# The order of work around the first block, and the place of one addend in the last batch entry, in a fused attention and FP4 feed-forward kernel

## The chip, the cores and the metric

The kernel runs on one core of a Trainium2 chip. A core has five engines, each with its own queue of instructions: TensorE (PE, matrix products), VectorE (DVE), ScalarE (ACT), GpSimd (POOL) and SyncE (SP, which issues the DMAs here). The metric is the device time of one execution in microseconds (us), as a median over runs.

## The reference, cut to what matters

The input `src` has 4 batch entries of 2048 rows of 256 values. Each row is normalized to `xn`, and two paths work on it: linear attention with a feed-forward layer, and a feed-forward layer in which each matrix product quantizes both of its operands to FP4 in groups of 16 values. The second is the gate of the first.

```python
xn = layernorm(src)
# path 1: linear attention (16 heads of 64), then an MLP
Q, K = elu(xn @ Wq + bq) + 1, elu(xn @ Wk + bk) + 1;  v = xn @ Wv + bv
KV = einsum('bshd,bshm->bhdm', K, v)          # sums over all 2048 rows of a batch entry
Z  = 1 / (einsum('bshd,bhd->bsh', Q, K.sum(1)) + 1e-6)
o  = einsum('bshd,bhdm,bsh->bshm', Q, KV, Z)
x1 = layernorm(xn + o @ Wo + bo) * g1 + be1
s  = layernorm(x1 + gelu(x1 @ W1 + b1) @ W2 + b2) * g2 + be2
# path 2: fp4(t) = round each group of 16 to a grid of 8 levels times its scale max|t|/6
h  = silu(fp4(xn) @ fp4(w_gate).T) * (fp4(xn) @ fp4(w_up).T)     # 704 wide
g  = silu(fp4(h) @ fp4(w_down).T)
return src + s * g
```

## The kernel before, in words

Rows are taken in blocks of 256 (two tiles of 128), 8 blocks to a batch entry, 32 in all. Attention of a batch entry needs the sums over all of its keys first. So an intro (L966 to L1025) computes the keys of entry 0, tile by tile, and each block of entries 0 to 2 computes beside its own work a share of the next entry's keys. The last entry, blocks 24 to 31, has no next keys; its blocks are shorter and have an order of their own.

*From keys to M.* Per half of the heads, `m_of_half` (L540 to L615) folds the sums of keys and values with Wv and Wo into a matrix M, so that a block needs only one product with its queries (`pa`, L825). It is a generator of steps: load Wv and Wo (one buffer each, so the second half's load of Wo waits for the first half's product with it); the key sums as a row (`pks`), through memory to all partitions (`ksum`); then `kcol` and `kh`; `pkv` and `kv`; and `pm`, which ACT copies to `m`. `step(gen, k)` runs k steps of such a generator.

*A block's FP4 path.* The scales of groups of x and h (`scales_x`, `scales_h`, L631 and L650) are made on DVE for block n while block n−1 runs. `spread_scales` (L666) transposes the scales on PE (`pscale`), ACT copies them (`scaleT`), SP stores them to memory and reads them back with eight broadcasting DMAs into `qT`. `grid_of_x` and `grid_of_h` round to the grid, `grid_T` (L683) transposes it by a DMA into `gridT`, and `quantized_x` and `quantized_h` (L691, L697) multiply the two on DVE: `qT` then holds the quantized operand. x of block n+1 and h of block n go through this together. From `qT`, `gate_up(n+1)` (`pg`, 32 matmuls, L702) makes the next block's h, and `down(n)` (`pd`, L727) this block's gate: ACT makes `g` by a silu, and `o` and `x` are allotted beside it, `x` loaded.

*A block's attention path.* `q_of` (`pq`, L763) makes `zq`, the queries; `sums` (L791) makes `pz`, its reciprocal `z`, and spreads it by memory to `zb`; `qz` (L818) multiplies `zq` by `zb`; `attention` makes `pa` and `x1`; `x1_T` transposes it (`pt_x`), `ffn_1` (`pf`), `ffn_2` (`py`) and `output` (L924) follow, the last two in the next block. `output` ends with two `scalar_tensor_tensor` that write `o` and take the addend in `o` and `g`.

*The weights.* w_gate and w_up are quantized tile by tile within the intro. w_down has two halves, `quantize_down(w, k)` (L350): maxima, scales, rounding on DVE and ACT over 128x704, then six transposes on PE (`pwd`) and copies by ACT to `wd`; the generator stops between these. W2 is multiplied in a form with fewer products, which needs four sums or differences of its quarters: `w2_sums` (L193), four POOL operations over 128x512. In the intro the quarters are loaded with tile 5 (`later`).

*POOL's addends.* POOL keeps the key sums (`kacc`), the small powers that make `rstd` (L379), and the addends: `gate_addend` (L748: `o = g·be2 + x`, `g = g·g2`, three passes over 128x512), `ffn_addend` (L755, two passes over x1) and `attention_addend` (xn + bo).

*What sets the order.* PE runs strictly in program order (L98 to L102). DVE and ACT do so until `in_order[0] = False` (L1046); behind that a scheduler orders DVE, ACT, POOL and SP by readiness, within explicit hints:

```python
with tc.issue_after(pool["last"]) if behind else nullcontext():   # L750
```

puts what stands in it behind the named instruction; `pool["last"]` is the last POOL addend issued so far. With `behind=False` the scheduler is free. The transition from intro to block 0 (L1026 to L1056) is an order written out by hand: the steps of w_down's quantization, of `gate_up(0)` and of M lie in each other's gaps.

Of the kernel before, what the change touches and what calls it, by code (L numbers as in the profile page):

```python
# [22 lines left out]
def linear_attention_gated_by_fp4_ffn(  # L23
# [40 lines left out]
    ND = D // P  # L64
# [128 lines left out]
    def w2_sums():  # L193
        nc.gpsimd.tensor_tensor(w2("t3"), w2("22"), w2("t1"), ALU.subtract)
        nc.gpsimd.tensor_tensor(w2("t1"), w2("t1"), w2("11"), ALU.subtract)
        nc.gpsimd.tensor_tensor(w2("t2"), w2("22"), w2("t1"), ALU.subtract)
        nc.gpsimd.tensor_tensor(w2("t4"), w2("21"), w2("t2"), ALU.subtract)
# [152 lines left out]
    def quantize_down(w, k):  # L350
        yield from quantize_weight(w[:, k, :], I, f"wd_{k}")
        for i0 in range(0, NI, 4):
            n = min(4, NI - i0)
            pt = mm_tile(f"pwd_{k}_{i0}")
            for i in range(n):
                cols = slice((i0 + i) * P, min((i0 + i + 1) * P, I))
                wide = cols.stop - cols.start
                tr(pt[:wide, i * P : (i + 1) * P], w[:, k, cols], ident)
            for lo, hi, rows_ in ((0, n, P),) if i0 + n < NI else ((0, n - 1, P), (n - 1, n, TAIL)):
                scalar.copy(  # L360
                    wd[:rows_, i0 + lo : i0 + hi, k * P : (k + 1) * P],
                    pt[:rows_, lo * P : hi * P].rearrange("p (i t) -> p i t", t=P),
                )
        yield


    pool = {}
# [282 lines left out]
    def scales_h(n, j):  # L650
        blk[n]["rs_h", j] = fp4_scale(blocks(blk[n]["h"][j]), scale[:, : I // BLK, j], f"h_{n}_{j}")

    def grid_of_h(n, j, issue=None):
        h3 = blocks(blk[n]["h"][j])
        fp4_grid(
            h3, blk[n].pop(("rs_h", j)), h3, [(blocks(grid_h[:, j, :I]), 0, I // BLK)],
            f"h_{n}_{j}", issue,
        )
# [7 lines left out]
    def spread_scales(n, h, x):  # L666

        cs = chunks_of(h, x)
        wide = cs.stop - cs.start
        ptT = mm_tile(f"pscale_{n}")[:, :P]  # L670
        tr(ptT, scale.rearrange("p k j -> p (k j)"), ident)
        sT = work.tile([P, P], F32, tag="scaleT", name=f"scaleT_{n}", bufs=1)
        scalar.copy(sT, ptT)
        s_d = dram.tile([P, P], F32, tag="scale_d", name=f"scale_d_{n}", bufs=2)
        nc.sync.dma_start(s_d, sT)
        by_block = s_d.rearrange("(c k j) t -> k c (j t)", c=NCH, j=TB)
        for k in range(P // BLK):
            nc.sync.dma_start(
                qT[k * BLK : (k + 1) * BLK, cs, :],
                by_block[k : k + 1, cs, :].to_broadcast([BLK, wide, T]),  # L680
            )
# [63 lines left out]

    def gate_addend(n, behind=True):  # L748
        g, o, x = (blk[n][k] for k in ("g", "o", "x"))
        with tc.issue_after(pool["last"]) if behind else nullcontext():  # L750
            nc.gpsimd.tensor_tensor(o, g, rows["be2"], ALU.mult)
            nc.gpsimd.tensor_tensor(o, o, x, ALU.add)
            pool["last"] = nc.gpsimd.tensor_tensor(g, g, rows["g2"], ALU.mult).ins
# [198 lines left out]
    def step(gen, times=1):  # L952
        for _ in range(times):
            next(gen, None)
# [70 lines left out]
            xn = xn_next  # L1025
    load_xn(1)  # L1026
    load_xnT(0)
    down_0, down_1 = (quantize_down(w_down_sb, k) for k in range(ND))
    step(down_0)
    step(gate, 2)  # L1030
    step(m_0)
    step(down_0)
    step(gate, 2)
    step(m_0)
    step(down_0)
    scales_x(1)
    step(gate)
    step(m_0)
    step(gate)
    scales_h(0, 0)  # L1040
    m_half = m_of_half(0, 1)
    step(m_half)
    step(gate, 9)
    step(m_0)
    scales_h(0, 1)
    in_order[0] = False  # L1046
    step(down_1)
    for sub in range(2):
        keys_in(1, sub)
    spread_scales(0, True, True)  # L1050
    step(down_1)
    w2_sums()
    for j in range(TB):
        grid_of_h(0, j)
    grid_of_x(1)
    grid_T(0, 0, NCH * TB)  # L1056

# [4 lines left out]
    def keys_beside(n):  # L1062
        return n // NB + 1 < B
# [10 lines left out]
    for n in range(NBLK):  # L1074
        b, bi = divmod(n, NB)
        subs = (2 * bi, 2 * bi + 1) if b + 1 < B else ()
        if n < last:
            gate = gate_up(n + 1)
        for sub in subs if n == 0 else ():
            keys_T(b + 1, sub)  # L1080
        if n > 0 and keys_beside(n - 1):
            gate_addend(n - 1)
        if subs:
            step(m_half)
            q_of(n)
            step(down_1)
            load_xnT(n + 1)
            kk_ins = keys_k(b + 1, subs[0])
            block_addends(n)
            with tc.issue_after(kk_ins):  # L1090
                ins = quantized_x(n)
            with tc.issue_after(sums(n, ins.ins).ins):
                for j in range(TB):
                    quantized_h(n, j)
            if n > 0:
                keys_T(b + 1, subs[1], keys["exp"])
            step(m_half)
            keys_xk(b + 1, subs[0])
            step(gate, 9)
            step(m_half)  # L1100
            down(n, 0)
            down(n, 1)
        elif n < last:
            def values():
                quantized_h(n, 0)
                return quantized_x(n)

            step(m_half)
            q_of(n, values)
            block_addends(n)  # L1110
            quantized_h(n, 1)
            load_xnT(n + 1)
            down(n, 0)
            sums(n)
            step(m_half)
            step(gate, 9)
            step(m_half)
            down(n, 1)
            gate_addend(n, False)
        else:  # L1120
            for j in range(TB):
                quantized_h(n, j)
                down(n, j)
        with tc.issue_after(blk[n + 1]["late"]) if n < last else nullcontext():
            qz_ins = qz(n)
        if not subs:
            ffn_2(n - 1, 4 if n < last else 8)
        kk_ins = keys_k(b + 1, subs[1]) if subs else qz_ins
        if n > 0:
            with tc.issue_after(kk_ins):  # L1130
                ffn_sums(n - 1)
        attention(n)
        if n + 2 < NBLK:
            load_xn(n + 2)
        if subs:
            keys_xk(b + 1, subs[1])
            if subs[1] % NB == NB - 1:
                m_half = m_of_half(b + 1, subs[1] // NB)
                step(m_half)
        bn, bin_ = divmod(n + 1, NB)  # L1140
        next_subs = (2 * bin_, 2 * bin_ + 1) if bn + 1 < B else ()
        for sub in next_subs if n > 0 else ():
            keys_in(bn + 1, sub)
        if n > 0:
            ffn_2(n - 1, 20)
        more = n + 1 < NBLK, n + 2 < NBLK
        if more[0]:
            scales_h(n + 1, 0)
            with tc.issue_after(qz_ins) if not subs else nullcontext():
                scales_h(n + 1, 1)  # L1150
            if more[1]:
                scales_x(n + 2)
        for sub in next_subs if n == 0 else ():
            keys_in(bn + 1, sub)
        for sub in next_subs[:1]:
            keys_apart(bn + 1, sub)
        if n == last:
            gate_addend(n)
        x1_T(n)
        if not subs:  # L1160
            ffn_addend(n, n == last)
        for sub in next_subs[1:]:
            keys_apart(bn + 1, sub, blk[n]["act"])

        if n > 0 and not subs:
            ffn_2(n - 1, 26)
        if more[0]:
            spread_scales(n + 1, *more)
        if n > 0:
            ffn_2(n - 1, 28)  # L1170
        if more[0]:
            grid_of_h(n + 1, 0)
            grid_T(n + 1, 0, NI)
            grid_of_h(n + 1, 1, blk[n]["act"])
            if more[1]:
                grid_of_x(n + 2, blk[n]["act"])
                if not subs:
                    attention_addend(n + 2, False)
            grid_T(n + 1, NI, (NCH if more[1] else NI) * TB)
        if n > 0:  # L1180
            output(n - 1)
        if n + 1 == last:
            q_of(last)
            ffn_1(n, range(NF // 2))
            sums(last)
            ffn_1(n, range(NF // 2, NF))
        else:
            ffn_1(n)
        for sub in next_subs[:1]:
            keys_T(bn + 1, sub, blk[n]["gelu"])  # L1190
# [38 lines left out]
```

## Time and profile before

| what | value |
|---|---|
| median of 3 runs | 1930.21 us (1927.91 to 1932.57) |
| the profiled execution | 1929.81 us |
| its span in the profile | 1927.7 us |
| mean granted TensorE clock | 0.996 |
| PE busy, of the span | 1892.9 us |
| DVE busy | 1495.7 us |
| POOL busy | 561.1 us |
| block 0's `pg` starts (intro's end) | 131.37 us |
| block 1's `pg` starts | 172.31 us |
| block 0's `pd` starts | 183.58 us |
| last block's `pf` starts | 1905.56 us |

In the lines of the profile a name such as `pg<-wgu,qT` is output and inputs by the program's tiles, followed by shapes and a count of equal neighbours that are shown as one line. The number ahead of the engine is the duration, or the stretch that all of them took; the bracket is the engine's idle time just before, and what ended it. L115 is the line of the helper through which all of DVE's and ACT's instructions are issued, L99 and L102 those of matmuls and transposes, so there the tile's name tells the place. "Granted clock" is the share of full speed that TensorE was given: at 0.5 a matmul takes twice its time.

### The profile page before, as it was taken

How to read it: one execution, taken by the hardware profiler on the slowest of the kernel's cores; microseconds unless marked ns; L12 is line 12 of the kernel's file. 1: busy time of each engine (PE TensorE's matmuls, PEld its weight loads, DVE VectorE, ACT ScalarE, POOL GpSimd, SP SyncE). 2: the span in 40 equal slices, each digit the busy share in tenths (PEclk: the TensorE clock that was granted, in tenths of full speed). 3: DMA queues.
4: the chain of work that ended last, by engine and by line, in shares of the span. 5: the costliest groups of instructions: out<-in, count | busy, mean ns of one | idle time of the engine just before them, and what ended most of it. 6: DMA issues, size and time to landing. Idle time of an engine off the chain costs nothing. (4 is left out here: it accounts for less than half of the span.)

```text
span 1927.7 us, 24464 instructions
## 1 busy us (share of the span) xinstructions
PE 1892.9 (98%) x8788; PEld 1380.7 (72%) x8788; DVE 1495.7 (78%) x2554; ACT 803.0 (42%) x1384; POOL 561.1 (29%) x461
## 2 busy tenths in 40 slices
PE   9999999999999999999999999999999999999997
PEld 4446677767777767777767777767777678788876
DVE  7878687777778877877777878877778788788775
ACT  2334554334444345443334554444443334444441
POOL 4441332232332233322232323232323232222221
PEclk9999999999999999999999999999999999999999
DMA  5435555454435445535244554455343244455431
GB/s 160 140 94 119 115 104 113 97 107 94 93 59 98 117 94 119 142 73 107 78 89 75 126 111 96 96 115 120 82 88 70 62 87 82 86 90 89 85 78 36
DMA packets 225121, 187.12 MB, mean 97 GB/s; under 512 B 103364, under 2 KB 185568, under 8 KB 225000
## 3 DMA queue, kind: packets, MB, share of 16 engines
q1 hardware_dynamic: 224168, 183.99, 45.0%
q8 instruction: 69, 1.13, 0.3%
q10 hardware_dynamic: 832, 1.57, 0.3%
q14 instruction: 52, 0.43, 0.1%
HBM read 131.41 MB, written 31.54 MB: 85 GB/s over the span
## 5 line engine op out<-in xcount | busy, mean ns | idle before, releaser
L508 POOL TENSOR_TENSOR kacc<-kacc,kk 128x512 f32<-128x512 f32 x120 | 178.9, 1491 | 591.2 <-DVE kk L115 589.1
L99 PE MATMUL pg<-wgu,qT 128*128 128x352 f32 x1024 | 310.4, 461 | 0.8 <-issue 0.3
L99 PEld LDWEIGHTS pg<-wgu,qT 128*128 128x128 f32 x1024 | 193.2, 190 | 119.9 <-issue 14.2
L99 PE MATMUL pxk<-kk,xn_k 128*128 128x512 f32 x512 | 237.7, 603 | 3.7 <-DVE kk L115 3.5
L99 PE MATMUL pa<-m,zq 128*128 128x256 f32 x1024 | 227.9, 380 | 5.2 <-DVE zq L115 5.2
L99 PE MATMUL pk<-wk_sb,xnT_k 128*128 128x512 f32 x512 | 230.4, 593 | 1.4 <-ACT xnT_k L115 1.0
L99 PE MATMUL pq<-xnT,wq_sb 128*128 128x256 f32 x1024 | 227.0, 380 | 0.2 <-ACT hT L115 0.2
L99 PE MATMUL pf<-x1T,w_sb 128*128 128x256 f32 x1024 | 227.0, 380 | 0.0
L379 POOL TENSOR_TENSOR rstd<-rstd,neg_half 128x2 f32<-128x2 f32 x96 | 73.0, 760 | 526.8 <-DVE rstd L115 477.6
L99 PEld LDWEIGHTS pa<-m,zq 128*128 128x128 f32 x1024 | 193.4, 190 | 43.8 <-issue 12.0
L99 PEld LDWEIGHTS pq<-xnT,wq_sb 128*128 128x128 f32 x1024 | 194.9, 191 | 27.1 <-ACT hT L115 0.6
L99 PEld LDWEIGHTS pf<-x1T,w_sb 128*128 128x128 f32 x1024 | 192.4, 190 | 25.6 <-issue 0.4
L115 ACT ACT_TABLE_LOAD x122 | 156.5, 1283 | 68.1 <-DVE k L115 55.3
L99 PE MATMUL pd<-wd,qT 128*128 128x256 f32 x768 | 172.3, 379 | 1.5 <-DVE qT L115 1.5
L99 PEld LDWEIGHTS pxk<-kk,xn_k 128*128 128x128 f32 x512 | 92.7, 190 | 110.3 <-issue 77.1
L99 PEld LDWEIGHTS pk<-wk_sb,xnT_k 128*128 128x128 f32 x512 | 97.2, 190 | 103.5 <-issue 96.8
L99 PEld LDWEIGHTS pd<-wd,qT 128*128 128x128 f32 x768 | 145.8, 190 | 25.9 <-DVE qT L115 2.3
L115 DVE SCALAR_TENSOR_TENSOR zq<-e,q 128x512 f32<-128x512 f32 x128 | 88.8, 704 | 70.2 <-ACT e L115 70.2
L115 ACT ACTIVATE h<-pg 128x352 f32<-128x352 f32 x128 | 58.7, 459 | 192.9 <-PE pg L99 192.8
L115 ACT ACTIVATE x1T<-pt_x,bcol 128x256 f32<-128x256 f32 x64 | 32.6, 560 | 255.4 <-PE pt_x L102 255.4
L115 ACT ACTIVATE ek<-k,neg_one 128x512 f32<-128x512 f32 x128 | 89.8, 719 | 113.1 <-DVE k L115 112.7
L115 ACT ACTIVATE hT<-pf,bcol 128x256 f32<-128x256 f32 x256 | 105.2, 471 | 67.0 <-PE pf L99 66.6
(133 smaller groups left out, 2824.9 us busy)
## 6 DMA issues: line engine op xcount, KB each, us to landing
zb<-z_d SPq DMA_DIRECT2D x128, 256.0 KB, 6.1
qT<-scale_d SPq DMA_DIRECT2D x248, 128.0 KB, 5.4
x_k<-in_L_attn_src_dram SPq DMA_DIRECT2D x32, 256.0 KB, 4.3
x<-in_L_attn_src_dram SPq DMA_DIRECT2D x32, 256.0 KB, 2.7
xn_d<-xn_k SPq DMA_DIRECT2D x32, 256.0 KB, 3.7
xn<-xn_d SPq DMA_DIRECT2D x32, 256.0 KB, 2.7
xnT_d<-xnT_k SPq DMA_DIRECT2D x32, 256.0 KB, 2.0
xnT<-xnT_d SPq DMA_DIRECT2D x32, 256.0 KB, 3.1
```

The source lines that it names most:

```text
L99: return tc.keep_in_program_order(nc.tensor.matmul(*args, **kw))
L115: ins = op(*args, **kw)
L379: pool["last"] = nc.gpsimd.tensor_tensor(rstd[:, j0:j1], rstd[:, j0:j1], neg_half[:, j0:j1], ALU.pow).ins
L508: acc = nc.gpsimd.tensor_tensor(kacc, kacc, kk, ALU.add)
```

## The change

It moves instructions and adds or removes none, and consists of four pieces.

1. *Transition.* All eight steps of `gate_up(0)` and block 0's scales now stand ahead of the second half of M's first products and ahead of all of w_down's quantization. M's first half stops before `pm`, which moves into block 0 behind `q_of`.
2. *Block 0.* w_down's quantization follows `quantized_x` there, by a hint, its transposes stand just ahead of `down(0)`. `keys_T` comes behind `q_of`.
3. *W2's sums* move from the transition (where the scheduler had placed them in the intro, as soon as W2 had arrived) into block 0 behind the addends.
4. *Last batch entry.* `gate_addend(n)` of blocks 24 to 30 was called at the end of block n's own `down`, without a hint; it is now called at the head of block n+1, behind the last POOL addend. In block 31, `x1_T` and `ffn_addend` come ahead of `gate_addend`, and `ffn_addend` is without a hint.

```diff
-    def gate_addend(n, behind=True):
+    def gate_addend(n):
         g, o, x = (blk[n][k] for k in ("g", "o", "x"))
-        with tc.issue_after(pool["last"]) if behind else nullcontext():
+        with tc.issue_after(pool["last"]):
...
-    down_0, down_1 = (quantize_down(w_down_sb, k) for k in range(ND))
-    step(down_0)
-    step(gate, 2)
+    down_steps = [quantize_down(w_down_sb, k) for k in range(ND)]
+
+    step(gate, 4)
     step(m_0)
-    step(down_0)
-    step(gate, 2)
-    step(m_0)
-    step(down_0)
+    scales_h(0, 0)
     scales_x(1)
-    step(gate)
-    step(m_0)
-    step(gate)
-    scales_h(0, 0)
+    step(gate, 4)
+    scales_h(0, 1)
     m_half = m_of_half(0, 1)
     step(m_half)
-    step(gate, 9)
-    step(m_0)
-    scales_h(0, 1)
+    step(m_0, 2)
+    spread_scales(0, True, True)
     in_order[0] = False
-    step(down_1)
     for sub in range(2):
         keys_in(1, sub)
-    spread_scales(0, True, True)
-    step(down_1)
-    w2_sums()
     for j in range(TB):
         grid_of_h(0, j)
+    step(m_half)
     grid_of_x(1)
     grid_T(0, 0, NCH * TB)
...
-        for sub in subs if n == 0 else ():
-            keys_T(b + 1, sub)
-        if n > 0 and keys_beside(n - 1):
+        if n > 0:
             gate_addend(n - 1)
         if subs:
-            step(m_half)
+            if n > 0:
+                step(m_half)
             q_of(n)
-            step(down_1)
+            if n == 0:
+                for sub in subs:
+                    keys_T(b + 1, sub)
+                step(m_0)
...
             block_addends(n)
+            if n == 0:
+                with tc.issue_after(pool["last"]):
+                    w2_sums()
             with tc.issue_after(kk_ins):
                 ins = quantized_x(n)
...
+            with tc.issue_after(ins.ins):
+                for g in down_steps if n == 0 else ():
+                    step(g, 2)
...
             step(gate, 9)
             step(m_half)
+            for g in down_steps if n == 0 else ():
+                step(g)
             down(n, 0)
             down(n, 1)
...
             down(n, 1)
-            gate_addend(n, False)
...
+        x1_T(n)
+        if not subs:
+            ffn_addend(n, False)
         if n == last:
             gate_addend(n)
-        x1_T(n)
-        if not subs:
-            ffn_addend(n, n == last)
```

## The prediction

> **What bounds the kernel now.** First the page's busy times:
>
> ```profile
> PE 1892.9 (98%) x8788; PEld 1380.7 (72%) x8788; DVE 1495.7 (78%) x2554; ACT 803.0 (42%) x1384; POOL 561.1 (29%) x461
> ```
>
> TensorE (PE) is idle for 1927.7 − 1892.9 = 34.8 us of the span, and the change touches no matmul. So it can win only such idle time, or time lost at a lowered clock, and the question is where both lie. The windows of 50 us on PE give: 6.4 us idle in 100–150, 2.5 in 150–200, some 1.5 in all of 200–1550, 10.7 in 1550–1900, 10.2 in the last 28. These are the places that the change touches: the transition into block 0, and the last batch entry (blocks 24 to 31). The timeline of PE, then those of SP, POOL and DVE, say what ends each gap. Transition:
>
> ```profile
> 151.84 0.48 PE L102 MATMUL pscale<-ident,scale 128*128 128x128 f32 x1 [3.81 <-DVE scale L115]
> 172.31 9.71 PE L99 MATMUL pg<-wgu,qT 128*128 128x352 f32 x32 [0.31 <-issue]
> ```
> ```profile
> 155.09 3.73 SPq L678 DMA_DIRECT2D qT<-scale_d  x8
> 163.03 2.69 SPq L687 DMA_TRANSPOSE gridT<-grid  x1
> ```
>
> Columns: start, duration, engine, line, operation, in brackets the idle time ahead and its releaser. Read: a stall of 3.81 us for the scales of block 0, and later a start of pg(1), block 1's gate matmuls, with no stall: the transposed grid (gridT) was there. The windows on PE show what such a stall costs besides (columns: window, length, PE busy, granted clock, DMA share, GB/s):
>
> ```profile
> 114.00:117.40 3.40, 3.40 (x5) 0.52 0.55 208
> 151.80:155.00 3.20, 3.16 (x12) 0.50 0.18 64
> 1889.00:1893.00 4.00, 3.82 (x17) 1.00 0.00 1
> 1902.00:1905.50 3.50, 3.44 (x19) 0.61 0.00 0
> ```
>
> They follow stalls of 2.64, 3.81, 1.58 and 1.45 + 1.01 us (with one short transposing between the last two). The Trainium skill ("TensorE: Matmul & The Clock Gate", section "Part 1: The HAM clock gate (the "warmup" mystery)") puts the price at an idle window of about 3.4 us. By that rule only the 3.81 would be charged; the rows charge the 2.64 and the split 2.5 too, so I take 2.5 as the point from which some 3.4 us at half clock, 1.7 us lost, must be expected.
>
> **Step 1, W2's four sums leave the intro.** They stand on POOL between the key sums and a rstd that DVE waits for:
>
> ```profile
> 102.62 1.60 POOL L197 TENSOR_TENSOR w_sb<-w_sb 128x512 f32<-128x512 f32 x1
> 104.19 1.15 POOL L379 TENSOR_TENSOR rstd<-rstd,neg_half 128x2 f32<-128x2 f32 x1
> ```
> ```profile
> 84.20 0.69 DVE L115 TENSOR_TENSOR k<-pk,bk 128x512 f32<-128x512 f32 x1 [0.88 <-PE pk L99]
> 91.14 0.68 DVE L115 SCALAR_TENSOR_TENSOR kk<-ek,k 128x512 f32<-128x512 f32 x1
> ...
> 98.90 0.69 DVE L115 TENSOR_TENSOR k<-pk,bk 128x512 f32<-128x512 f32 x1 [3.09 <-PE pk L99]
> 108.16 0.68 DVE L115 SCALAR_TENSOR_TENSOR kk<-ek,k 128x512 f32<-128x512 f32 x1
> ```
>
> From the first k to the third kk the tile before took 6.94 us, this one 9.26: **2.3 us** are the sums' price (queue on POOL, and stretched DVE operations beside them). In the intro DVE is the chain up to pg at 131.37, so I carry all of it. Bounds: 0 (other work fills it) to 3. Behind the attention addends of block 0 POOL stands idle in before from 173.2 to 194.3, and takes the four passes (1.27 each) there; beside DVE they stretch one or two operations, 0.6 us, counted in step 2.
>
> **Step 2, the transition and block 0.** I use before's clock of time, unshifted. In front of the scales PE now has all eight gate groups, pks and pkv, no w_down transposes. From pg at 131.37: four times eight gates at 2.5 from start to start, two pks at 0.95, pkv at 1.1, so PE is through at 144.4. The scales on DVE need the last gate (142.4), h 0.52, its maximum 0.88 and a scaling 0.18, with ACT and queueing about 144.9 (w_down's quantization no longer stands between): a gap of 0.5, too short to lower the clock, instead of 3.81. Then pscale 0.3, pq 7.1 (the page's 227.0/32 at full clock), pt_k 1.2, pm_0 1.9, so 155.4; then pk 3.7, pz 1.0, pkv 1.1, pxk 3.6 (less the overlaps): PE reaches pg(1) at 164.5 instead of 172.3.
>
> But SP now carries a new wait. In the built order the load of Wo for the second half stands between the second and third of the eight qT broadcasts, and it needs the one Wo buffer, free when pm_0 ends (155.4); before, that load was issued at 148.06 ahead of the whole chain. Behind it queue six broadcasts and the gridT transpose. Six issues at 3.73/8 take 2.8 us, so gridT is issued at 158.7. In before it was issued at 163.03 and its consumer, the qT product on DVE, started at 171.21: 8.2 us. That gives 166.9, and with 0.9 for the product 167.8. The last batch's chain shows 9.3 for the same transfer: 168.0. So PE stands 3.3 us before pg(1), above my 2.5: half clock behind it.
>
> What is late next is w_down: both halves' quantization (ten passes over 128x704 at 0.82 to 0.88 us, two small reciprocals) now follows quantized_x on DVE, mixed with z (0.42 + 1.75), qT (1.76) and the h products. Added row by row, w_down's first half is done 13.95 us behind gridT, the second 16.05, and 0.6 for the sums beside them: 183.55. Six transposes (0.82) and the copy by ACT put pd at 184.8, against 183.58 for pd in before: **+1.2**; with the 9.3 us transfer +2.3. The half clock under pg(1) is hidden by that DVE train. I take **+1.7**. Bounds: −4.6, if gridT's wait vanishes and w_down follows in time; +5, if pd starts at half clock behind stalls of 1.6 and 1.9 us and the train is stretched.
>
> **Step 3, the gate addend of blocks 24 to 30 moves into the next block.** In before its three POOL passes run while DVE makes zq, and PE waits for zq (block 26):
>
> ```profile
> 1711.56 1.22 DVE L115 TENSOR_TENSOR zq<-zq,zb 128x1024 f32<-128x1024 f32 x1 [1.01 <-DMA zb<-z_d]
> 1713.93 2.29 DVE L115 TENSOR_TENSOR zq<-zq,zb 128x1024 f32<-128x1024 f32 x1
> 1716.29 5.45 PE L99 MATMUL pa<-m,zq 128*128 128x256 f32 x24 [0.69 <-DVE zq L115]
> ```
>
> Beside POOL the second zq takes 2.29 for 1.22, and the gaps before pa are 0.63, 0.69, 0.56, 0.74 and 1.05 us at 1670, 1715, 1760, 1806 and 1853: **3.7 us** to win. In its new place the addend stands behind the rstd of the previous block's output, beside the o pair. Three batches of before show that place already:
>
> ```profile
> 270.54 2.89 DVE L115 SCALAR_TENSOR_TENSOR o<-s,rstd,o 128x256 f32<-128x256 f32 x2 [0.58 <-POOL rstd L379]
> ...
> 1691.66 0.88 DVE L115 SCALAR_TENSOR_TENSOR o<-s,rstd,o 128x256 f32<-128x256 f32 x2 [0.59 <-POOL rstd L379]
> 1694.83 0.96 DVE L115 TENSOR_TENSOR qT<-qT,gridT 128x768 f32<-128x768 f32 x1 [2.28 <-DMA qT<-scale_d]
> ```
>
> Here the Trainium skill speaks against the change ("SBUF — State Buffer", section "Who interferes with whom": a VectorE instruction with two SBUF inputs contends with a GpSimd one that reads SBUF, and whoever is second is blocked for the whole instruction). By the rule alone the collision is only moved: each of the two o passes could wait one POOL pass of 1.40 us, +2.8 per block, about what was won or more. The row says +2.0 (2.89 against 0.88), and behind the pair DVE stands idle for 2.03 to 4.28 us before its next qT product. That idle time takes the 2.0; what remains is a qT or a zq caught by the last pass. Block by block I estimate 0.4, 0, 0.15, 0.4, 0.5 and 0 for 25 to 30, and 1.0 to 1.3 for 31 (1871.66), where three zq follow at once and delay pz: **2.75**. Bounds: 0, or 2.0 in each of seven blocks.
>
> **Step 4, the last block's tail.** POOL now takes x1's passes ahead of the gate's, so x1's normalization loses its neighbour:
>
> ```profile
> 1899.32 2.68 DVE L115 TENSOR_SCALAR x<-x,mv,rstd 128x256 f32<-128x256 f32 x2 [0.21 <-POOL rstd L379]
> 1902.06 0.55 PE L102 MATMUL pt_x<-ident,x 128*128 128x128 f32 x3 [1.01 <-DVE x L115]
> ```
>
> Elsewhere that pair takes 0.73 (1679.30): −1.95. The split stall then falls under 2.5, and the half clock behind it, 1.25 more, goes: pf from 1905.56 to about 1902.4, **−3.2**, at least −1.95. The gate's passes end well before the last output needs them.
>
> **Sum.** −2.3 + 1.7 − 3.7 + 2.75 − 3.2 = −4.7. The profiled execution took 1929.81 (span 1927.7 + 2.1), 0.4 below the median of 1930.21. So 1929.8 − 4.7 = 1925.1, against the median **1925.5**.
>
> **Rivals.** 0.2% (3.9 us) is about what a measurement of this kernel can tell from no change, so the bounds are 1926.4 and 1934.1.
> 1. *Gains are swapped for waits.* The front's 2.3 is eaten behind gridT, the 3.7 by the moved collisions; the tail alone stays: about 1927.5, "same". For it: every gain is under 1 us but the tail's. Against: the DVE idle before qT.
> 2. *The front's gain stands whole.* gridT lands by the time PE reaches pg(1), and w_down's train keeps pace: −4.6 − 2.3 − 4.1 = −11, about 1919. Against: one Wo buffer.
> 3. *Slower: the moved addend in the last batch.* Each of seven blocks pays the whole 2.0 us, since the stretched o pair pushes qT, pg and, in PE's fixed order, all behind: 14 − 3.7 − 3.2 − 0.6 (front) = +6.5, about 1936.5. It decides from (3.9 + 7.5)/7 = 1.6 us per block. For it: the pair's row. Against: the idle 2.03 to 4.28.
> 4. *The change doesn't do what it says*: the built order puts the sums and addends where I described them, so no chance is kept for this.
>
> **How the numbers follow.** Forecast (−2.5 to −7) 0.45, of which 0.35 lies under 1926.4; rival 1: 0.22; rival 2: 0.15; rival 3: 0.18. Faster 0.35 + 0.15 = 0.50; same 0.10 + 0.22 = 0.32; slower 0.18. The range 1918.5 to 1934.0 takes in rivals 1 and 2 and leaves out rival 3.
>
> **What would show it.** Step 1: third kk of the seventh tile about 7 us behind its first k. Step 2: pscale's gap under 1.3 with clock 1.0 behind it; the Wo load in the midst of the qT broadcasts; a gap of about 3 us before pg(1), with a low clock; pd about 0.6 us earlier than before in all (step 1 included). Step 3: no gap before pa in blocks 25 to 29, o pairs of 2.9, the idle before qT shrunk. Step 4: x pair 0.73. Wrong: gridT more than 10 us in flight, a DVE train far over 16 us, or gaps at pz and pg in the last batch.

## The result and the profile after

The changed kernel takes **1924.1 us** (median of 10 runs, 1922.63 to 1924.93), against 1930.12 for the kernel before in the same series (10 runs, 1926.1 to 1932.57). The ratio is 0.9971, with a 95% interval of 0.9961 to 0.9981. That is 5.6 us by the ratio (3.7 to 7.5 by its interval) and 6.0 between the medians: more than the 3.9 us (0.2%) that the prediction took as the least that can be told from no change, though the near end of the interval is not. The median lies 1.4 us below the forecast of 1925.5. The profiled execution took 1924.93 us, its span is 1923.1.

The page, first part:

```profile
PE 1892.4 (98%) x8788; PEld 1379.4 (72%) x8788; DVE 1495.0 (78%) x2554; ACT 804.0 (42%) x1384; POOL 552.9 (29%) x461
```

PE is as busy as before, to 0.5 us; what was won is idle time (30.7 us for 34.8). To see where, I take the same matmul group in both profiles and subtract its start in before. This is the **lead table**: us, negative is earlier, in brackets the start of the group in before. Each row is one profiled execution; the kernels are described below.

| kernel | keys of tile 1 (15.8) | end of intro (124.5) | block 0's pa (192.2) | block 23's pf (1541.7) | block 30's pf, first half (1872.4) | second half (1876.9) | block 31's pf (1905.6) |
|---|---|---|---|---|---|---|---|
| the change | +1.75 | −0.56 | +1.27 | +1.30 | −3.55 | −1.19 | −4.19 |
| e1_sums | +0.05 | −2.26 | −1.77 | −1.75 | −2.47 | −2.47 | −2.40 |
| e2_last | +0.10 | +0.28 | −0.54 | −0.51 | −5.65 | −3.29 | −6.56 |
| e3_front | +1.74 | +1.67 | +3.80 | +3.85 | +2.13 | +2.13 | +0.69 |
| e4_wo_late | +2.08 | −0.21 | −0.62 | −0.56 | −5.73 | −3.37 | −6.50 |
| e5_tail | −0.01 | +0.41 | −0.03 | −0.01 | −0.90 | −0.90 | −4.11 |
| e6_sums_last | +1.48 | −0.83 | −1.83 | −1.79 | −7.13 | −4.78 | −7.88 |
| e9_sums_gap | −0.05 | −2.35 | −5.71 | −5.67 | −10.29 | −7.94 | −11.27 |
| e10_half_early | +1.87 | −0.43 | −3.25 | −3.22 | −6.22 | −3.86 | −7.01 |
| e11_block31 | +0.19 | −2.11 | −0.28 | −0.24 | −3.30 | −3.30 | −4.73 |
| e13_gate | +1.89 | +2.16 | +3.24 | +3.24 | −2.11 | +0.25 | −0.99 |
| e14_best | +0.05 | −2.25 | −7.04 | −7.06 | −10.82 | −8.47 | −11.71 |

Between block 0's pa and block 23 no row moves by more than 0.07 us: those 1350 us are PE's alone, and nothing done at the front is given back there.

*The start.* Six profiles are 1.5 to 2.1 us late before anything that differs has run. The windows on PE show it for the change as a granted clock of 0.76 between 10 and 15 us, where before has 1.00. Six of the twelve new profiles have it, and kernels with the same front are on both sides (the change and e11_block31, e13_gate and e5_tail). So it belongs to the execution and not to the kernel (more on it under the clock threshold), and I count leads from the first column on.

*Step 1* in the change, POOL's and then DVE's timeline:

```profile
103.07 0.70 POOL L379 TENSOR_TENSOR rstd<-rstd,neg_half 128x2 f32<-128x2 f32 x1 [2.15 <-DVE rstd L115]
```
```profile
100.65 0.69 DVE L115 TENSOR_TENSOR k<-pk,bk 128x512 f32<-128x512 f32 x1 [2.13 <-PE pk L99]
...
107.60 0.68 DVE L115 SCALAR_TENSOR_TENSOR kk<-ek,k 128x512 f32<-128x512 f32 x1
```

The rstd that stood in POOL's queue in before now waits for DVE itself, and from the first k to the third kk the tile takes 6.95 us.

*Step 2*, PE's timeline, then SP's:

```profile
144.19 0.30 PE L102 MATMUL pscale<-ident,scale 128*128 128x128 f32 x1 [0.56 <-DVE scale L115]
...
168.74 11.76 PE L99 MATMUL pg<-wgu,qT 128*128 128x352 f32 x32 [5.35 <-DVE qT L115]
...
184.74 5.45 PE L99 MATMUL pd<-wd,qT 128*128 128x256 f32 x24 [0.46 <-ACT wd L115]
```
```profile
147.91 0.80 SPq L678 DMA_DIRECT2D qT<-scale_d  x2
154.27 0.40 SPq L134 DMA_DIRECT2D wo<-in_L_attn_Wo_dram  x1
154.71 2.87 SPq L678 DMA_DIRECT2D qT<-scale_d  x6
157.68 8.09 SPq L687 DMA_TRANSPOSE gridT<-grid  x1
```

The stall at the scales is gone, and a longer one stands ahead of pg(1). SP shows what may be its cause (e4 below tests it): two broadcasts, then nothing for 5.6 us until the one Wo buffer is free, then the other six and gridT. Behind the stall the windows on PE give half clock:

```profile
168.74:172.14 3.40, 3.40 (x6) 0.50 0.71 231
```

*Steps 3 and 4.* The stretch of DVE that answers to the zq lines of the prediction, then the place where an addend now is, ahead of it, then the last block, all on DVE's timeline. (The matmul groups, counted from the first block, show that those lines belong to block 27; the prediction called it 26, and its five gaps belong to blocks 26 to 30.)

```profile
1714.35 1.22 DVE L115 TENSOR_TENSOR zq<-zq,zb 128x1024 f32<-128x1024 f32 x1
```
```profile
1691.89 2.90 DVE L115 SCALAR_TENSOR_TENSOR o<-s,rstd,o 128x256 f32<-128x256 f32 x2 [0.59 <-POOL rstd L379]
1694.99 2.34 DVE L115 TENSOR_TENSOR qT<-qT,gridT 128x768 f32<-128x768 f32 x2 [0.20 <-DMA qT<-scale_d]
```
```profile
1868.12 2.90 DVE L115 SCALAR_TENSOR_TENSOR o<-s,rstd,o 128x256 f32<-128x256 f32 x2 [0.59 <-POOL rstd L379]
1870.94 2.96 DVE L115 SCALAR_TENSOR_TENSOR zq<-e,q 128x512 f32<-128x512 f32 x3
...
1898.41 0.73 DVE L115 TENSOR_SCALAR x<-x,mv,rstd 128x256 f32<-128x256 f32 x2 [0.23 <-POOL rstd L379]
```

zq takes 1.22 us for 2.29, and the five gaps ahead of pa are gone. The o pair takes 2.90, and the idle time behind it has shrunk from 2.28 to 0.20 us: it took the stretch, as reckoned. In the last block there is no idle time behind the pair; the three zq take 2.96 for 1.89, and PE's timeline shows two new stalls ahead of pz, this one and one of 0.59 us at 1875.16:

```profile
1872.84 1.74 PE L99 MATMUL pz<-zq,kh 128*32 128x256 f32 x12 [0.41 <-DVE zq L115]
```

### The profile page after: what moved, and what is told of

It reads as the page before. It is cut to its first block, busy times and chain, and to the rows that moved or that the text cites. A ratio compares the mean times of both kernels' runs of the same rounds, so it can differ in the third digit from the quotient of the medians.

```text
span 1923.1 us, 24467 instructions
## 1 busy us (share of the span) xinstructions
PE 1892.4 (98%) x8788; PEld 1379.4 (72%) x8788; DVE 1495.0 (78%) x2554; ACT 804.0 (42%) x1384; POOL 552.9 (29%) x461
```

## The experiments

Times are medians of 5 to 12 runs, ratios are to the kernel before in the same series. The diffs are cut to the lines that matter, against the kernel that is named.

**e1_sums: before, with W2's sums alone moved.**

```diff
-    w2_sums()
...
             block_addends(n)
+            if n == 0:
+                with tc.issue_after(pool["last"]):
+                    w2_sums()
```

> Before, with W2's four sums alone moved behind the addends of block 0. Theory: in the intro they cost 2.3 us of DVE's chain (the profiles' lag of the change from before falls from +1.75 to -0.56 between the keys of tile 6 and pg), and nothing takes it back: pg of block 0 at about 129.1 us if the start is like before's, pd of block 0 2.3 us earlier, total -2.3 (about 1927.8). Rival: the transition's scales wait for work that does not come earlier, so the gap ahead of pscale grows by what was won: pd of block 0 where it was, total 0.

Measured: 1925.93 us, ratio 0.9978 (0.9968 to 0.9988). In the lead table the intro gives −2.31, so the theory's 2.3 holds there. Behind it 0.49 is given back up to block 0's pa, but that is no measure of the rival: e6, with the same code up to there, wins another 1.00, and the three others with before's transition (e2, e5, e13) lie between −0.82 and +1.08. They differ in the clock behind the scales' stall, which was lowered in before, e1 and e13 and not in e2, e5 and e6. The times show more (4.3, interval 2.3 to 6.2) than the profile's 2.6 in span; the chance terms at the start and at the stalls are the likely difference, which single profiles cannot settle.

**e2_last: before, with the last batch entry alone** (steps 3 and 4 of the change, as in its diff).

> Before, with the last batch entry of the change alone (gate addends of blocks 24 to 30 in the next block, block 31's x1 passes ahead of the gate's). Theory: blocks 24 to 30 give 4.9 us up to pf of block 30, block 31's first half takes 2.4 back (pz gaps), the tail gives 3.0 to 3.4: total -5.5 to -6 (about 1924.4), the lag constant at 0 up to 1550 us. Rival: only the tail gains, the rest is due to another phase of the queues behind the altered front: total -3 (1927).

Measured: 1924.6 us, ratio 0.9970 (0.9959 to 0.9981). The lead from block 23's pf: −5.14, then +2.36, then −3.27, together −6.05. The theory holds term by term.

**e3_front: transition and block 0 alone** (the change's diff at L1028 to L1100, with `w2_sums()` in the transition and the last entry as before).

> The change's transition and block 0 alone (W2's sums and the last batch entry as before). Theory: pscale's gap falls from 3.8 to about 0.6 us, but pg(1) waits 5 us for gridT and runs at half clock, and pd of block 0 comes 1.7 us late: total +1.7 (about 1931.9). Rival: block 0's loss in the change comes from W2's sums beside DVE, which are not there now: pd within 0.3 us of before's, total 0.

Measured: 1929.86 us, ratio 0.9997 (0.9987 to 1.0007). The lead from the intro's end to block 0's pa: +2.13, behind a stall of 5.17 us ahead of pg(1). So the loss is the reordering's, and W2's sums have no part in it. The times say −0.6 (−2.5 to +1.4), a little better than the profile's step; what makes up for it in this profile is the end (no half clock in block 31, −1.4).

**e4_wo_late: the change, with Wo's second load behind gridT** (`late[0]` is the second half's `load_when(dep, wo, ...)`, held back until here).

```diff
     grid_T(0, 0, NCH * TB)
+    with tc.issue_after(transposed[0].ins):
+        late[0]()
```

> The change, with the load of Wo's second half issued behind the gridT transpose instead of amid the qT broadcasts. Theory: SP's wait on the one Wo buffer (from 148.7 to 154.3) is the cause of the gap of 5.35 us ahead of pg(1); without it gridT is issued at about 153.5, lands at 162, pg(1) starts by 164 without a gap and at full clock, DVE's train with w_down moves along, and pd of block 0 starts at about 179.5 instead of 184.7: total -5 against the change (about 1919). Rival: w_down's quantization on DVE sets pd whatever gridT does, so that the gap only moves behind pg(1): total 0 to -1 against the change (1923.5).

Measured: 1922.89 us, ratio 0.9959 (0.9944 to 0.9974). The stall ahead of pg(1) falls from 5.35 to 0.18 us, so SP's wait was its cause; but the lead from the intro's end to block 0's pa improves from +1.83 to −0.41, by 2.2 and not by 5. Neither number was right. PE's and DVE's timelines show why:

```profile
173.12 5.51 PE L99 MATMUL pg<-wgu,qT 128*128 128x352 f32 x12 [3.03 <-DVE h L115]
```
```profile
166.68 3.64 DVE L115 TENSOR_TENSOR qT<-qT,gridT 128x768 f32<-128x768 f32 x2
```

The stall has moved into pg(1), where it waits for DVE, and DVE's train is longer than in the change: qT's pair took 3.64 us for 1.76. W2's sums run beside it. In the change the same sums ran from 164.12 to 169.82, mostly while DVE waited for gridT, and the last (168.15 to 169.82) beside z and the maxima of w_down, which took 0.42 and 0.88 us, as in e9 without a neighbour.

**e9_sums_gap: e4, with W2's sums in the idle time behind the intro.**

```diff
+    with tc.issue_after(pool["last"]):
+        w2_sums()
     step(gate, 4)
...
-            if n == 0:
-                with tc.issue_after(pool["last"]):
-                    w2_sums()
```

> As e4 (Wo's second load behind gridT), with W2's sums behind the intro's last key sum, where POOL and DVE are both idle, instead of in block 0. Theory: in e4 the sums ran beside DVE's qT pair (3.64 us for 1.76) and the maxima of w_down (1.24 for 0.18), 2.9 us of the train that sets pd; without them pg(1)'s inner gap of 3.0 us shrinks to about 0.5 and pd of block 0 comes 2.9 us earlier than in e4 (at about 180.0 if the start is the same): total -2.5 to -3 against e4 (about 1920). Rival: the stretch was not on the path, since PE would wait for w_down's transposes just as long: total 0 against e4.

Measured: 1919.75 us, ratio 0.9948 (0.9936 to 0.9961). The step from the intro's end to block 0's pa is −3.36, that is 2.95 us better than e4. DVE's timeline:

```profile
164.53 1.76 DVE L115 TENSOR_TENSOR qT<-qT,gridT 128x768 f32<-128x768 f32 x2
```

The rival fails: the stretch was on the path.

**e10_half_early: e9, with w_down's first half ahead of block 0's h.**

```diff
+    step(down_steps[0], 2)
     step(gate, 4)
...
-                for g in down_steps if n == 0 else ():
+                for g in down_steps[1:] if n == 0 else ():
                     step(g, 2)
```

> As e9, with the quantization of w_down's first half on DVE ahead of block 0's h products, in the idle 6.5 us behind the intro. Theory: DVE's train from gridT to w_down's second half is the bound of pd; 5 us shorter, PE becomes the bound and pd of block 0 comes another 3 to 4 us earlier, while pscale is delayed by under 1.5: total -3 against e9 (about 1917). Rival: the half in front delays the scales (pscale, scale_d, qT, gridT) by as much as it saves later, and is stretched by the sums beside it: total 0 against e9.

Measured: 1921.19 us, ratio 0.9953 (0.9940 to 0.9965); the step is −2.82, 0.5 worse than e9. The rival holds here, and the form in which it does is seen on DVE:

```profile
130.56 1.43 DVE L115 SCALAR_TENSOR_TENSOR w_down<-w_down,rs_wd 128x704 f32<-128x704 f32 x1
132.85 2.90 DVE L115 SCALAR_TENSOR_TENSOR w_down<-m_wd,w_down 128x704 f32<-128x704 bf16 x2 [0.86 <-ACT m_wd L115]
135.79 1.84 DVE L115 TENSOR_TENSOR w_down<-w_down,am_wd 128x704 f32<-128x704 f32 x1
```

Beside the sums these took 6.17 us, where 3.5 (4 × 0.88) are their own; h, the gates behind it (a gap of 1.33) and pscale (1.04 for 0.56) came later.

**e14_best: e10, with the sums at the end of block 0 instead** (the two lines that e9 added are gone; the sums stand behind `x1_T(n)`, for n = 0, and POOL runs them from 200.5 to 210.7 us).

> As e10, but W2's sums at the end of block 0, so that w_down's first half is quantized in the idle time behind the intro without a neighbour. Theory: e10 lost 2.7 us there to the sums (5.9 us for 3.5), of which some 2 reached pscale; pscale and all behind it come 2 us earlier than in e10, pd is then bound by PE or nearly: lead over before at block 0's pa, less the start's, -7 (e9: -5.7, e10: -5.1), total about 1.3 under e9's (1918.5). Rival: pd's bound is PE's own order of work (pg, pm, the transposes and their copies), so that nothing is left to win: as e9; or the sums stretch block 0's normalizations at the end of the block: over e9.

Measured: **1918.0 us**, ratio 0.9936 (0.9922 to 0.9949), clearly better than the change; it is the lowest of all medians, with an interval that overlaps e9's. The theory's lead of −7 at block 0's pa came out (−7.1 less the start), and block 0's end lost nothing (−7.06 at block 23). The three lines above now read:

```profile
128.75 0.89 DVE L115 SCALAR_TENSOR_TENSOR w_down<-w_down,rs_wd 128x704 f32<-128x704 f32 x1
130.50 1.82 DVE L115 SCALAR_TENSOR_TENSOR w_down<-m_wd,w_down 128x704 f32<-128x704 bf16 x2 [0.85 <-ACT m_wd L115]
132.35 0.89 DVE L115 TENSOR_TENSOR w_down<-w_down,am_wd 128x704 f32<-128x704 f32 x1
```

The step is −4.79, 1.4 better than e9. Ahead of pd PE now stands still for 1.6 us in all, in two gaps.

**e6_sums_last: the change without its reordered transition** (e1 and e2 together).

> Before, with W2's sums later and the last batch entry of the change, but before's own transition and block 0 order. Theory: the parts add, since they lie 1400 us apart: -2 (front, after the transition has given 0.5 back) and -5 to -6 (last entry) by the traces, about 1922 to 1923, so at or under the whole change: the reordered transition is then no gain. Rival: the change's order of block 0 is needed to keep the sums' gain, total -5 only (1925).

Measured: 1921.64 us, ratio 0.9957 (0.9943 to 0.9971): the theory. In the lead table, less the start, −9.4 at block 31's pf, against −5.9 in the change.

The times of the three parts do not add up to the change: −4.3 (e1), −5.8 (e2) and −0.6 (e3) are −10.7, where the change won 5.6. An estimate says where the excess lies. A run's span times the missing part of its granted clock is the time that it lost at a lowered clock: on average 8.1 us for before in the series of e1 to e3, 5.6 for e1, 5.3 for e2, 7.2 for e3, and, in other series, 6.0 for the change and 3.1 for e6. The rest of the mean time, less that of before, is −1.8, −2.8 and +0.7 us for the parts, together −4.0, and −4.4 for the change. By this estimate the time at full clock adds up, and what does not is the time at a lowered clock.

**e5_tail and e13_gate: before, with the last entry in its two parts.**

```diff
+        x1_T(n)
+        if not subs:
+            ffn_addend(n, False)
         if n == last:
             gate_addend(n)
-        x1_T(n)
-        if not subs:
-            ffn_addend(n, n == last)
```

is e5_tail, and

```diff
-        if n > 0 and keys_beside(n - 1):
+        if n > 0:
             gate_addend(n - 1)
...
             down(n, 1)
-            gate_addend(n, False)
```

is e13_gate.

> Before, with block 31's order alone (x1's passes ahead of the gate's on POOL, x1's addend without a hint). Theory: x1's normalization takes 0.73 for 2.68 us; the second half of block 31 (from its second group of pf to the tail's pf) comes 1.7 to 2.0 earlier where before runs it at full clock, 3.1 where before has a half clock there: total -1.7 to -3.3 (about 1927.5). Rival: the tail gain in the whole change came from the earlier addend of block 30, not from the order: total 0.

> Before, with the gate addends of blocks 24 to 30 in the next block, block 31's order as before. Theory: up to pf of block 30 it gives 4.6 to 5.3 us against the profile of before, of which 0.7 to 1.7 come without it too (the two other profiles with the old last entry), then 2.4 are lost in block 31: net -1 to -2.5, total about 1928.5. Rival: the loss in block 31 eats all, or zb's round trip hides the whole: total 0.

Measured: 1926.76 us, ratio 0.9986 (0.9977 to 0.9995), and 1928.44 us, ratio 0.9985 (0.9977 to 0.9994). In e5_tail the second half of block 31 gives −3.21, in the profile with the half clock as reference. In e13_gate blocks 24 to 30 give −5.35, block 31 takes 2.36 back, and the end gives −1.24 without any change in its order. Both theories hold in the profiles; the two effects are separate, and their ratios multiply to 0.9971, against 0.9970 for e2_last.

**e11_block31: the change, with block 30's addend where before had it.**

```diff
-        if n > 0:
+        if 0 < n < last:
             gate_addend(n - 1)
...
             down(n, 1)
+            if n + 1 == last:
+                gate_addend(n, False)
```

> The change, but block 30's gate addend stays where before had it (in block 30, without a hint). Theory: in the last block the addend beside the o pair and three zq costs PE 2.4 us (two pz gaps of 0.41 and 0.59, and the lost lead), which comes back; block 30's stall ahead of pa returns in part (0.6 to 1.0): total -1.4 against the change (about 1922.7). Rival: the last block has idle time behind pz anyway (6.9 us of DVE, waiting for zb), so that the 2.4 us were lost to zb's round trip and not to the addend: total +0.5 to +1 against the change.

Measured: 1922.39 us, ratio 0.9963 (0.9951 to 0.9975). The 2.36 us of block 31 come back whole (−3.30 in both columns). But up to there blocks 24 to 30 give 3.06 for 4.85, and behind it pa waits 2.01 us for zb, with this clock after it (windows on PE):

```profile
1886.30:1889.70 3.40, 3.40 (x11) 0.65 0.00 0
```

Less the start, block 31's pf is at −4.9, against −5.9 in the change; the times lie the other way, with intervals that overlap. Whether this place is better stays open.

## Why the prediction was right

The time (1924.1 for 1925.5), its direction and every step's sign came out. Term by term, in the profile pair of before and after:

| term | predicted | measured |
|---|---|---|
| start (chance) | 0 | +1.75 |
| step 1, intro | −2.3 | −2.31 |
| step 2, to block 0's pa | +1.7 | +1.83 |
| step 3, to block 30's pf | −3.7 + 1.45 | −4.85 |
| step 3, block 31 | +1.3 | +2.36 |
| step 4, tail | −3.2 | −3.00 |
| behind block 31's pf | 0 | −0.41 |
| sum | −4.7 | −4.6 |

That −4.6 lies so near to −4.7 is luck in part: without the late start the pair gives −6.35, and the terms below were off in both directions. Two of the prediction's own signs of being wrong appeared as well: gridT was more than 10 us in flight, and PE waits at pz in the last block.

**Step 1** was right in mechanism and size: all eight profiles of kernels without the sums in the intro show −2.29 to −2.31, and the four others with them lie between −0.07 and +0.42.

**Step 2** came out in its sum, +1.83 (again +1.83 in e11), by luck: two of its terms were off and made up for each other. The stall ahead of pg(1) was put at 3.3 us and is 5.35, since gridT took 10.3 us from its issue to DVE's product, not 8.2 to 9.3. The 8.2 was never the transfer's time. In before DVE took the product up without any idle time, as soon as it had done kv; only in the change did it wait for the DMA (DVE's timeline, before and after):

```profile
171.21 0.89 DVE L115 TENSOR_TENSOR qT<-qT,gridT 128x512 f32<-128x512 f32 x1
```
```profile
167.99 0.69 DVE L115 TENSOR_TENSOR qT<-qT,gridT 128x512 f32<-128x512 f32 x1 [5.43 <-DMA gridT<-grid]
```

The records of the DMA packets agree. The 2048 packets of 256 bytes that make up gridT move from 164.20 to 168.34 us in before, and only from 162.25 to 167.41 in the change, 4.6 us behind the issue, where Wo's load and six broadcasts had been issued in the 3.4 us just before it. In e4, which moves Wo's load behind and nothing else, they move 1.9 us behind the issue, and gridT lands after 6.5 us. So the late Wo cost twice: it delayed the issue of gridT, and it left more on the queue ahead of it.

In return DVE's train from that product to w_down's second half took 15.3 us, not 16.65. The 0.6 for W2's sums fell away, since they ran in DVE's wait; the rest is probably the adding row by row: the durations of the train's rows sum to 16.9 us, but each row begins some 0.08 us before the one ahead of it ends. That the wait for Wo is the cause of the stall was shown (e4); that the train with w_down sets pd behind it was shown as well (e4, e9, e14). Rival 2, that the front's gain stands whole, was refuted by the stall.

**Step 3** had the right mechanism and a wrong size in both terms. Block 31's cost was put at 1.0 to 1.3 and is 2.36, in all eight kernels that have the addend there; e11 shows that it is the addend. The costs of blocks 25 to 30 were put at 1.45 and do not show: PE's stalls ahead of pz and pd from block 23's to block 30's pf sum to 3.51 us, and to 3.71 in before. The idle time ahead of qT took them. And part of what was won is not the change's. The stalls ahead of pa, which were the gain to be had, sum to 3.67 us in the profile of before, but to 1.37, 1.80 and 2.74 in e1, e3 and e5, with the *old* last entry; these gain 0.72, 1.72 and 0.89 us over before up to block 30's pf. So the profile on which the 3.7 rests was an unfavourable one. The new order gives 3.0 to 5.35, on average 4.65 in eight profiles; six of them have no such stall, two have one of 0.33 and 0.37. So it is worth some 3.5 to 3.8 us to that point (4.65 less the mean of those three, or of all four with before), and 1.2 to 1.5 when block 31 has taken its 2.36. Rival 3, the slower case, fails: the o pair did take 2.90 us, but in six of seven blocks with cover. Rival 1, that the gains are swapped for waits and only the tail's stays, missed with its 1927.5, but not by much in its mechanism: of the front's 2.31 us 0.48 stay, and of the moved addend's 4.85 us 2.49.

**Step 4** came out at −3.0, and at −3.21 alone (e5). Its second part, the half clock in before's tail, was taken as part of the mechanism. It is chance, of a kind that the next paragraph explains: with the same stalls of 1.45 and 1.01 us, e3_front and e13_gate show no lowered clock there and are 1.4 and 1.2 us ahead of before. The order alone is worth about 1.9.

**The clock threshold** was the wrong rule in the working. I read 2.5 us from before's rows. The experiments have the same stalls with both outcomes: 2.64 us with the clock at 0.53 (before) and at 1.00 (e2, e3); 3.81 with 0.50 (before, e13) and 1.00 (e5); 3.25 with 1.00 (e6) beside 3.23 with 0.50 (e1); and 2.01 with 0.65 (e11). The clock records of the traces tell why. A spell of half clock ahead of the last matmuls lasts 3.41 or 6.83 us, and within one execution all spells begin on one grid of 3.413 us (before: 114.17, 151.71 and 1902.75). The grid lies elsewhere in every execution. What counts is how long PE was busy in one window of the grid, not how long the stall was. Here is the stall of 3.81 us on the grid, first in before, where it fills a window, then in e5, where the grid cuts it in two (windows on PE; columns as in the prediction):

```profile
148.30:151.71 3.41, 0.00 (x0) 1.00 0.53 156
151.71:155.12 3.41, 3.28 (x13) 0.50 0.20 73
```
```profile
146.91:150.32 3.41, 1.52 (x8) 1.00 0.47 103
150.32:153.74 3.42, 1.50 (x12) 1.00 0.36 126
153.74:157.15 3.41, 3.41 (x17) 1.00 0.70 215
```

In all 13 profiles, from 10 us on, 7242 windows of the grid ran at full clock. In 22 of them PE was busy for at most 1.41 us (41%), and the next window ran at half clock every time. In the other 7220 it was busy for 1.46 us or more, and the clock stayed. So what lowers the clock is 2.0 us of idle time or more in one window: 2.01 in e11, and in before's tail the two short stalls together with 2.39. Worked out from these figures, as an estimate: a stall of less than 2.0 us that stands alone is not charged, one of 4.0 us or more always is, and one between is charged or not by where the grid lies. The late start goes with the grid too: the six late profiles have a window that begins between 5.3 and 6.3 us, the seven others none.

The Trainium skill ("TensorE: Matmul & The Clock Gate", section "Part 1: The HAM clock gate (the "warmup" mystery)") says that the window of about 3.4 us runs freely, so that what it catches depends on where it falls. These records agree. It asks for an idle window, though, and here one that was busy for 41% was enough.

## What to carry to other kernels

When a load waits for its buffer, what stands behind it on the same queue waits too, as six broadcasts and gridT did here for 5.6 us: look for it in the built order of the queue, and put it behind what the next stage needs. Work on POOL was free here where DVE was idle (e9) or ran rows that it did not stretch (z and the maxima in the change); beside other rows the same sums and addends cost 2.3 to 3 us (the intro, block 31, e4). The timeline names the neighbours before a move is tried; the amount was still misjudged in e4 (2.2 us for 5) and e10 (0.5 lost for 3 won). A difference of 1 to 2 us between two profiles can come from where the clock's grid lies: compare the same group of work in several profiles, stage by stage, before it is explained.

## What was not expected of the hardware

A stall of one length lowers TensorE's clock in one execution and not in the next (2.64, 3.81 us), and it then costs 1.2 to 1.7 us. It depends on a grid of 3.413 us: from 10 us on, half clock followed every full-clock window in which PE was busy for 1.41 us or less, and none with 1.46 or more. Two short stalls in one window count together (1.45 and 1.01 us in before's tail). A transposing DMA landed 10.3 us after its issue where Wo's load and six broadcasts had just been issued, and 6.5 us after it where Wo's load came behind (e4).
